# The products of the diffusion matrix in a two-layer graph kernel: one ordered list that runs ahead of its use, with the second step's results transposed and kept in DRAM

## The chip, the cores and the metric

The kernel runs on one core of one Trainium2 chip. The metric is the device time of the launch in microseconds. A profiled execution gives, besides, a trace of every instruction on the engines: TensorE (PE, matmuls and transposes; PEld is its weight load), VectorE (DVE), ScalarE (ACT), GpSimd (POOL) and SyncE (SP, which here only issues DMA transfers).

## The reference, cut to what matters

`x` is 2708x512 in fp32, `adj` 2708x2708 with entries 0 and 1. Layer 0 is a graph attention with 8 heads; it ends near 1050 us and neither kernel differs in it. Layer 1 is this, with `S = adj`, `U*` of 2x512x512 and `W*` projecting to 64 columns:

```python
S = S + eye(n)
Rf = S / clip(S.sum(axis=1, keepdims=True), 1e-12)
Rb = S / clip(S.sum(axis=0), 1e-12)[:, None]
Xf, Xb, Xa = (X, X, X)
Z = zeros_like(X)
for s in range(2):
    A = adj_from_feats(Xa, W1, W2, W3)      # logits (Xa W1) W2 (Xa W3)^T, then per row:
    Xf = Rf @ Xf                            # softmax, keep the largest entries up to a
    Xb = Rb @ Xb                            # mass of 0.9 (order decides ties), softmax
    Xa = A @ Xa                             # of what is kept
    Z = Z + (Xf @ U1[s] + Xb @ U2[s] + Xa @ U3[s])
Y = X + Z                                   # then a layer norm of Y; the layer's input is added
```

Both `Rf` and `Rb` are `S` with its rows scaled, so in step 1, where `Xf` and `Xb` are both `X`, one product `S @ X` serves both. In step 2 there are two, `S @ Xf` and `S @ Xb`.

## The kernel before, in words

**Tiles.** The 2708 rows are 22 row tiles of 128 (the last has 20). Two neighbouring tiles are a pair (`pairs`, 11), four are a quad (`quads`, 6, the last of two tiles). Each of the two steps is a pass over the pairs. Tiles are stored with 128 rows on the partitions.

**One pair in a step.** `Logits.queries` loads the queries; `Logits.products` (L517, L519) multiplies them with the resident `keys` and copies the logits to a tile `p` of 128x2708 (four buffers). `Logits.exp` gives the maxima (L544, VectorE), the exponentials in place (ACT), three thresholds to be looked at (`points`, GpSimd, which ends in the negated thresholds `nth`, L569) and, on ACT, two passes over `p` per threshold and tile, the looks (L549), which give the mass above it. `search` (VectorE) finds the threshold with further passes over `p` (`mass`, L624), writes the kept entries to `keep` and takes the largest of the rest (`finish`, L800 and L802), and branches at run time on whether ties or too few candidates need more work (L866 to L884); it ends in `rden`, the reciprocal of the kept mass (L901). `attended` transposes `keep` in groups of four blocks (L1004), copies them to `at` (L1008) and multiplies them with the resident values `va` (L1023); `rden` scales the result to `xa`. `mixed` (L1051) multiplies `xf`, `xb` and `xa`, each transposed first by `transposed` (L147, with the ACT copy at L149), with the blocks `u_k` of `U1`, `U2`, `U3`, which are loaded from DRAM every time. In step 1, `project` takes the transposed `xa` to next step's queries and keys in `kq_d`; the sum goes to `y_d`. In step 2, `y_d` is added and the layer norm follows: `moments` (L137 to L139) and two operations on VectorE in `normed` (L1083), and the store to `out`.

**`S`'s products.** `s_d` holds `S` transposed in DRAM. A product is computed in f32r with the right side split in two parts, `hl`, that sum to the fp32 value. `part(half, b)` returns a list of steps for half a quad. A step `product(c)` loads `hl` (L953, 512 KB) and a block `s_r` of `s_d` (L955, 256 KB) and issues two matmuls per row tile of the quad (L959) with 512 columns, into four PSUM tiles `q0` to `q3`. In step 1 one quad's 22 row blocks `c` are spread over two pairs; then `scaled` (L965) multiplies the result with 1/row sum and 1/column sum (`rinv`, `cinv`) on ACT, stores both to `xfb_d` (L966, issued by GpSimd) and calls `split_rows` (L181, L182 on VectorE; L183 stores to `fhl_d` or `bhl_d`), which makes the two parts for step 2. In step 2, `part` gives a quad's 22 blocks with `fhl_d` in one pair and with `bhl_d` in the next. `diffused` loads a pair's `xf` and `xb` from `xfb_d`.

**Order.** PE, ACT, DVE and SP run in the order in which the program issues (`manual_schedule`); GpSimd's order is set by a scheduler. While VectorE searches for pair g+1, the function `late` issues pair g's attention and `mixed` with two lists woven in by `paced`: `others` (the product steps) and `fills` (exponentials and looks of pair g+2). SP issues all loads in one order, and a load that waits for its buffer or its source holds those behind it.

**Start of a step.** Each step opens its own pools. It loads the keys, computes the first two pairs' logits, and runs eleven product blocks (step 1) or 22 (step 2) before `values` loads `va`, then more beside the first search. In step 2, `ranks` (L1099 to L1125) comes first: it gives each row its rank among rows with equal keys, for ties. It multiplies the keys with a ramp (L1103), copies to `same`, transposes, and counts with 22 passes of VectorE, eleven before the first logits and eleven after; `spread` sends the ranks to all partitions through DRAM.

Of the kernel before, what the change touches and what calls it, by code (L numbers as in the profile page):

```python
# [9 lines left out]
F32 = mybir.dt.float32  # L10
# [43 lines left out]
def kernel(  # L54
# [59 lines left out]
    xa_d = dram.tile([N, D], F32, name="xa_d")  # L114
    en_d = dram.tile([H, N], F32, name="en_d")
# [11 lines left out]
    ratio = const.tile([P, NT], F32, name="ratio")  # L127

# [13 lines left out]

    def transposed(pool, psum, src, pr, name):

        pt = psum.tile([P, KD, P], F32, name="t")
        for k in range(KD):
            nc.tensor.transpose(pt[:, k, :pr], src[:pr, k * P:(k + 1) * P], ident[:pr, :pr])  # L147
        dst = pool.tile([P, KD, P], F32, name=name)
        nc.scalar.copy(dst[:, :, :pr], pt[:, :, :pr])  # L149
        return dst  # L150
# [442 lines left out]
    def search(lg, looked, early, late):  # L593
# [110 lines left out]
        vn = small.tile([P, G, nx], F32, name="vn", bufs=1)  # L704
        sn = small.tile([P, G, nx], F32, name="sn", bufs=1)
        left = vec("left")
        eighth = small.tile([P, G, nx // 8], F32, name="eighth", bufs=1)
# [85 lines left out]
        def finish(go):  # L793
# [14 lines left out]
            rest = small.tile([P, G, nx], F32, name="rest", bufs=1)  # L808
# [95 lines left out]
    for s in range(STEPS):  # L904
        last = s == STEPS - 1
        with ExitStack() as st:
            big = st.enter_context(tc.tile_pool(name=f"s{s}big", bufs=1))
            wide = st.enter_context(tc.tile_pool(name=f"s{s}wide", bufs=2))
            sp = st.enter_context(tc.tile_pool(name=f"s{s}sp", bufs=4 if last else 3))
            work = st.enter_context(tc.tile_pool(name=f"s{s}work", bufs=2))  # L910
            up = st.enter_context(tc.tile_pool(name=f"s{s}u", bufs=4))
            parts = None if last else st.enter_context(tc.tile_pool(name=f"s{s}parts", bufs=2))
            small = st.enter_context(tc.tile_pool(name=f"s{s}small", bufs=2))
            ps_t = st.enter_context(tc.tile_pool(name=f"s{s}pst", bufs=2, space=PSUM))
            ps_a = st.enter_context(tc.tile_pool(name=f"s{s}psa", bufs=2, space=PSUM))
            ps_s = st.enter_context(tc.tile_pool(name=f"s{s}pss", bufs=1, space=PSUM))

            va = big.tile([P, NT, D], F32, name="va")

            keys = big.tile([P, N], F32R, name="keys")  # L920
            h = (NT - NT % G - G) * P
            for c in (slice(0, h), slice(h, N)):
                for i in range(2):
                    nc.sync.dma_start(out=keys[i * DA:(i + 1) * DA, c].bitcast(F32), in_=kq_d[s][:DA, i, c])
            rank = big.tile([P, N], BF16, name="rank") if last else None

            def values():
                for t in range(NT):
                    nc.sync.dma_start(out=va[:rows[t], t, :], in_=(xa_d if last else va_d)[cols[t], :])

            if last:
                g_b = big.tile([P, D], F32, name="g_b")
                nc.sync.dma_start(out=g_b, in_=row_bcast(gamma, D))

            def part(half, b):

                if b // 2 >= len(quads):  # L940
                    return []
                quad = quads[b // 2]
                first = b % 2 == 0
                w = len(quad) * P
                hl_d = (fhl_d if first else bhl_d) if last else vhl_d
                cs = range(NT) if last else range(0, NT // 2) if first else range(NT // 2, NT)
                steps = []

                def product(c):
                    if c == 0:  # L950
                        half[:] = [ps_s.tile([P, D], F32, name=f"q{i}") for i in range(len(quad))]
                    hl = sp.tile([P, 2, D], F32R, name="hl", bufs=3)
                    nc.sync.dma_start(out=hl.bitcast(F32), in_=hl_d[c * P:(c + 1) * P])  # L953
                    s_r = sp.tile([P, 2 * G * P], F32R, name="s_r")
                    nc.sync.dma_start(out=s_r[:, :w].bitcast(F32),  # L955
                                      in_=s_d[c * P:(c + 1) * P, quad[0] * P:quad[0] * P + w])
                    for j in range(len(quad)):
                        for h in range(2):
                            nc.tensor.matmul(half[j], lhsT=s_r[:, j * P:(j + 1) * P], rhs=hl[:, h],  # L959
                                             start=(c == 0 and h == 0), stop=(c == NT - 1 and h == 1))  # L960

                def scaled(t, ps, i, inv, to):
                    pr = rows[t]
                    x = work.tile([P, D], F32, name="xe")
                    nc.scalar.activation(x[:pr], ps[:pr], AF.Copy, scale=inv[:pr, t:t + 1])  # L965
                    nc.gpsimd.dma_start(out=xfb_d[i, cols[t], :], in_=x[:pr])  # L966
                    if not last:
                        split_rows(parts, nc.vector, x[:pr], t, to)

                steps += [lambda c=c: product(c) for c in cs]  # L970
                if last or not first:
                    for j, t in enumerate(quad):
                        if first or not last:
                            steps.append(lambda j=j, t=t: scaled(t, half[j], 0, rinv, fhl_d))
                        if not first:
                            steps.append(lambda j=j, t=t: scaled(t, half[j], 1, cinv, bhl_d))
                return steps

            def paced(steps, n):
                for step in steps[:n]:  # L980
                    step()
                del steps[:n]

            def diffused(grp):
                out_ = []
                for i in range(2):
                    for t in grp:
                        x = work.tile([P, D], F32, name=f"x{i}")
                        nc.sync.dma_start(out=x[:rows[t]], in_=xfb_d[i, cols[t], :])
                        out_.append(x)  # L990
                return out_[:len(grp)], out_[len(grp):]

            def attended(grp, keep, rden, fills, others, then):

                def turned(i, t, cs):
                    pr = rows[t]  # L1000
                    pt = ps_t.tile([P, TG, P], F32, name="t")
                    at = work.tile([P, TG, P], F32, name="at")
                    for j, c in enumerate(cs):
                        nc.tensor.transpose(pt[:rows[c], j, :pr], keep[i][:pr, cols[c]], ident[:pr, :pr])  # L1004
# [69 lines left out]
            def normed(t, y):  # L1074
# [10 lines left out]

                return rest

            def ranks():

# [148 lines left out]
```

## Time and profile before

| what | value |
|---|---|
| median of 3 runs | 3779.58 us (3772.61 to 3780.49) |
| the profiled execution | 3774.21 us, span of its instructions 3772.1 us |
| mean granted TensorE clock | 0.956 |
| layer 0, before 1050 us | PE busy 989.3, DVE 864.1, ACT 231.5, POOL 327.3 us |
| layer 1, step 1 (1050.0 to 2323.5 us) | PE 1101.8, DVE 636.4, ACT 655.5, POOL 254.6 us |
| layer 1, step 2 (2323.5 to 3772.0 us) | PE 1292.2, DVE 1110.7, ACT 653.1, POOL 256.4 us |
| DMA | 634 MB, 168 GB/s over the span; the DMA engines 50% busy |

The shares of busy time are averages over stages with different limits. The matmuls' ends in the trace are modelled and overlap, so the distance from one start to the next says more about a matmul's price than its listed duration. A group's line names the engine, the line of the kernel, output and input tiles, the count, then busy time and mean nanoseconds of one, then the idle time of the engine before the group and what ended it.

### The profile page before, as it was taken

Reading aid. Unit: us, or ns where it says so; the run is one execution under the profiler, and the core shown is the slowest. Engines: PE = TensorE matmul, PEld = TensorE weight load, DVE = VectorE, ACT = ScalarE, POOL = GpSimd, SP = SyncE. Lnnn points to the kernel's source line nnn. Section 1 sums busy time; section 2 is a strip of 40 time slices with the busy share of each in tenths; the row PEclk is TensorE's granted clock in tenths of the full one; section 3 lists DMA queues with packets and bytes.
Section 4 is the critical chain, followed back from the end, with each engine's and each line's share of the span. In section 5 each row is a group of like instructions: output and inputs, shape, how many; then the busy total and the mean of one; then the engine's idle time right before and its main releaser. Section 6 shows DMA issues by size and latency. Waiting matters only on the chain. (4 is left out here: it accounts for less than half of the span.)

```text
span 3772.1 us, 35425 instructions
## 1 busy us (share of the span) xinstructions
PE 3383.3 (90%) x11143; PEld 1760.6 (47%) x11143; DVE 2611.1 (69%) x4814; ACT 1540.1 (41%) x2334; POOL 838.2 (22%) x1187
## 2 busy tenths in 40 slices
PE   8999999999855898989898998668999999999988
PEld 4433333333533455545454453435555665556443
DVE  4588888989946526474554641967779798777992
ACT  2343202111025565546566621335544556445511
POOL 4115151423331121121212020302121211212101
PEclk9999999999977999999999998989999999999989
DMA  3476424233154554454545352845556665567552
GB/s 115 159 255 219 155 78 140 85 99 114 44 167 143 193 197 158 154 184 146 195 146 206 114 176 83 302 130 206 187 202 225 229 209 192 197 212 243 184 192 88
DMA packets 276457, 634.07 MB, mean 168 GB/s; under 512 B 37209, under 2 KB 70441, under 8 KB 273243
## 3 DMA queue, kind: packets, MB, share of 16 engines
q1 hardware_dynamic: 249183, 540.99, 43.3%
q0 software_dynamic: 27024, 90.30, 6.3%
q8 instruction: 89, 1.46, 0.2%
q14 instruction: 161, 1.32, 0.1%
HBM read 509.07 MB, written 122.10 MB: 167 GB/s over the span
## 5 line engine op out<-in xcount | busy, mean ns | idle before, releaser
L1023 PE MATMUL a<-va,at 128*128 128x512 f32 (+2 forms) x1936 | 898.0, 603 | 58.0 <-ACT at L1008 57.9
L959 PE MATMUL q<-hl,s_r 128*128 128x512 f32 x2904 | 821.8, 429 | 67.2 <-DMA s_r<-s_d 65.7
L429 PE MATMUL po<-e,fw 128*65 128x512 f32 (+4 forms) x2112 | 840.4, 553 | 30.0 <-DVE e L427 22.2
L427 DVE SCALAR_TENSOR_TENSOR e<-r_b,kk,a_c 128x512 f32<-128x512 f32 (+4 forms) x1056 | 752.3, 741 | 68.8 <-PE po L429 18.2
L959 PEld LDWEIGHTS q<-hl,s_r 128*128 128x128 f32 x2904 | 545.8, 190 | 312.4 <-issue 147.5
L549 ACT ACTIVATE junk_a<-p,nth 128x2708 uint8<-128x2708 f32 (+1 forms) x240 | 613.0, 2554 | 93.2 <-POOL nth L569 89.6
L429 PEld LDWEIGHTS po<-e,fw 128*65 128x65 f32 (+1 forms) x2112 | 286.5, 140 | 544.2 <-issue 269.1
L1023 PEld LDWEIGHTS a<-va,at 128*128 128x128 f32 (+2 forms) x1936 | 339.6, 188 | 428.2 <-issue 347.2
L1051 PE MATMUL a<-u_k,v_t 128*128 128x512 f32 (+1 forms) x1056 | 490.8, 601 | 20.9 <-ACT xa L1031 15.1
L624 DVE SCALAR_TENSOR_TENSOR junk<-p,th 128x2708 bf16<-128x2708 f32 (+1 forms) x132 | 402.2, 3047 | 4.0
L1008 ACT COPY at<-t 128x512 f32<-128x512 f32 (+3 forms) x308 | 139.8, 476 | 439.4 <-PE t L1004 439.2
L1051 PEld LDWEIGHTS a<-u_k,v_t 128*128 128x128 f32 (+1 forms) x1056 | 188.6, 186 | 239.6 <-issue 187.0
L517 PE MATMUL t<-keys,q_t 128*128 128x452 f32 x528 | 167.9, 444 | 117.0 <-ACT p L519 95.0
L800 DVE SCALAR_TENSOR_TENSOR keep<-p,th 128x2708 f32<-128x2708 f32 (+1 forms) x44 | 133.4, 3033 | 132.4 <-PE t L1004 131.1
L181 DVE TENSOR_SCALAR split_hl<-xe 128x512 int32<-128x512 int32 (+1 forms) x44 | 19.0, 432 | 275.6 <-ACT xe L965 232.6
L802 DVE MAX8 vn<-keep 128x8 f32<-128x2708 f32 (+1 forms) x66 | 196.8, 2981 | 2.3
L519 ACT COPY p<-t 128x452 f32<-128x452 f32 (+2 forms) x264 | 132.7, 539 | 149.8 <-DVEq L884 78.9
L517 PEld LDWEIGHTS t<-keys,q_t 128*128 128x128 f32 x528 | 91.8, 211 | 188.7 <-ACT p L519 149.5
L411 ACT ACTIVATE s_c<-a_c 128x512 fp32r<-128x512 f32 (+3 forms) x132 | 76.2, 577 | 248.3 <-DMA a_c<-in_adj_t_dram 123.2
L1004 PE MATMUL t<-ident,keep 128*128 128x128 f32 (+1 forms) x968 | 146.4, 273 | 21.9 <-DVE keep L752 16.5
L1004 PEld LDWEIGHTS t<-ident,keep 128*128 128x128 f32 (+1 forms) x968 | 114.5, 138 | 105.1 <-issue 76.9
L544 DVE TENSOR_REDUCE nmx<-p 128x1 f32<-128x2708 f32 (+1 forms) x44 | 129.2, 2966 | 40.3 <-ACT p L519 40.1
(294 smaller groups left out, 3105.1 us busy)
## 6 DMA issues: line engine op xcount, KB each, us to landing
s_r<-s_d SPq DMA_DIRECT2D x330, 256.0 KB
hl<-vhl_d SPq DMA_DIRECT2D x132, 512.0 KB
u_k<-in_L_gnn_U_dram SPq DMA_DIRECT2D x264, 256.0 KB
hl<-fhl_d SPq DMA_DIRECT2D x132, 512.0 KB
hl<-bhl_d SPq DMA_DIRECT2D x132, 512.0 KB
arow<-in_adj_dram SPq DMA_DIRECT2D x21, 1354.0 KB
s_d<-s_c SPq DMA_DIRECT2D x88, 256.0 KB
a_c<-in_adj_t_dram SPq DMA_DIRECT2D x84, 256.0 KB
```

The costliest lines, as they stand in the source:

```text
L427: nc.vector.scalar_tensor_tensor(e[:pr, :cw], r_b[:pr, i, :cw], kk[:pr, t, hd:hd + 1], a_c[t][:pr, :cw], op0=OP.max, op1=OP.mult)
L429: nc.tensor.matmul(po[i][:, :cw], lhsT=fw[:pr, t, hd, :], rhs=e[:pr, :cw], start=(t == 0), stop=(t == NT - 1))
L517: nc.tensor.matmul(pl[:, :c1 - c0], lhsT=q[:, i], rhs=self.keys[:, c0:c1], start=(i == 0), stop=(i == 1))
L549: nc.scalar.activation(junk[:pr], self.p[i][:pr], func, **kw)
L624: v.scalar_tensor_tensor(junk_b[:pr], ps_[i][:pr], th, ps_[i][:pr], op0=OP.is_ge, op1=OP.mult, accum_out=dst)
L800: v.scalar_tensor_tensor(keep[i][:pr], ps_[i][:pr], t, ps_[i][:pr], op0=OP.is_lt, op1=OP.mult, accum_out=left[:pr, i:i + 1] if e else None)
L802: v.max(vs, keep[i][:pr])
L959: nc.tensor.matmul(half[j], lhsT=s_r[:, j * P:(j + 1) * P], rhs=hl[:, h], start=(c == 0 and h == 0), stop=(c == NT - 1 and h == 1))
L1004: nc.tensor.transpose(pt[:rows[c], j, :pr], keep[i][:pr, cols[c]], ident[:pr, :pr])
L1008: nc.scalar.copy(at[:r, j0:j1, :pr], pt[:r, j0:j1, :pr])
L1023: nc.tensor.matmul(pa[:pr], lhsT=at[:rows[c], j, :pr], rhs=va[:rows[c], c, :], start=(c == 0), stop=(c == NT - 1))
L1051: nc.tensor.matmul(pz[i][:rows[t]], lhsT=v_t[i][:, k, :rows[t]], rhs=u_k, start=(n == 0 and k == 0), stop=(n == 2 and k == KD - 1))
```

## The change

A class `Products` holds one list of steps for both passes: in step 1's part per quad 22 `product` and one `scaled` per tile, in step 2's part per quad and per side (`Xf`, `Xb`) 22 `turned` and four `stored`. There are 466 steps. The driver takes a number of them for each pair, whichever pass they belong to. Two sets of 26 (one quad each) are taken at the start of step 1, before and beside the first search. The rest is spread over step 1's pairs so that step 2 keeps 32 for its start and 19 for each of ten pairs.

`turned` exchanges the operands of the matmul, so that the result comes out transposed, 512 row numbers of the quad along the free side. `stored` copies it to `xt_d` in DRAM without a scale. `diffused` loads it for a pair in step 2 and multiplies it, with `times` on GpSimd, by a row of `rinv` or `cinv` that `spread_scales` has written to `scale_d` and that is broadcast to all partitions. In step 1 `xb` is no longer transposed: it is the transposed `xf` times `ratio`. `split_rows` is gone from the products: `split` loads a stored tile from `xfb_d`, multiplies by 4097, subtracts twice for the upper part and once for the lower, all on GpSimd; seven splits are issued per pair in step 1.

The last pair of step 1 transposes and projects `xa` first; its `u` products, in the order `U3`, `U1`, `U2`, are issued in step 2's start. `ranks` becomes a class `Ranks` whose tiles are two of the `p` buffers: the keys of the first 18 tiles are loaded, and their ranks counted, beside the last pair of step 1; the other four tiles follow after the last keys. The pools are opened once for both steps; `s_r` has three buffers in both (before: 3 and 4), `u_k` three (3 and 4), the shared tiles `v_t` take both row tiles of a pair. Layer 0 is as before.

```diff
-            def part(half, b):
-                ...
-                cs = range(NT) if last else range(0, NT // 2) if first else range(NT // 2, NT)
-                ...
+        class Products:
+            def __init__(self):
+                self.steps, self.ready, self.splits, self.split_at = [], {}, [], 0
+                self.at = 0
+                for q, quad in enumerate(quads):
+                    self.steps += [lambda quad=quad, c=c: self.product(quad, c) for c in range(NT)]
+                    self.steps += [lambda t=t, j=j: self.scaled(t, j) for j, t in enumerate(quad)]
+                    self.ready[0, q] = len(self.steps)
+                for q, quad in enumerate(quads):
+                    for i in range(2):
+                        self.steps += [lambda quad=quad, i=i, c=c: self.turned(quad, i, c) for c in range(NT)]
+                        self.steps += [lambda quad=quad, q=q, i=i, k=k: self.stored(quad, q, i, k)
+                                       for k in range(KD)]
+                    self.ready[1, q] = len(self.steps)
+            ...
+            def turned(self, quad, i, c):
+                while (i, c) not in self.splits[:self.split_at]:
+                    self.split(1)
+                hl, s_r, w = self.operands((fhl_d, bhl_d)[i], quad, c)
+                for k in range(KD):
+                    for h in range(2):
+                        nc.tensor.matmul(self.half[k][:, :w], lhsT=hl[:, h, k * P:(k + 1) * P], rhs=s_r[:, :w],
+                                         start=(c == 0 and h == 0), stop=(c == NT - 1 and h == 1))
+
+            def stored(self, quad, q, i, k):
+                w = len(quad) * P
+                x = work.tile([P, D], F32, name="xe")
+                nc.scalar.copy(x[:, :w], self.half[k][:, :w])
+                nc.gpsimd.dma_start(out=xt_d[q, i, :, k, :w], in_=x[:, :w])
+
+            def split(self, n):
+                for i, t in self.splits[self.split_at:self.split_at + n]:
+                    self.split_at += 1
+                    ...
+                    nc.gpsimd.dma_start(out=x, in_=xfb_d[i, cols[t], :])
+                    nc.gpsimd.tensor_scalar(x4[:pr], x, 4097.0, None, op0=OP.mult)
+                    nc.gpsimd.tensor_tensor(high, x4[:pr], x, op=OP.subtract)
+                    nc.gpsimd.tensor_tensor(high, x4[:pr], high, op=OP.subtract)
+                    nc.gpsimd.tensor_tensor(x, x, high, op=OP.subtract)
+                    nc.gpsimd.dma_start(out=(fhl_d, bhl_d)[i][t * P:(t + 1) * P], in_=hl)
...
+        def times(dst, v, r, i, w):
+            nc.gpsimd.tensor_tensor(dst[:, :, :w], v[:, :, :w], r[:, i, :w].unsqueeze(1).to_broadcast([P, KD, w]),
+                                    op=OP.mult)
...
+                x = up.tile([P, KD, G * P], F32, name="v_t")
+                nc.sync.dma_start(out=x[:, :, :w], in_=xt_d[q, i, :, :, c0 * P:c0 * P + w])
+                times(x, x, r, i, w)
...
+        BEGUN, AHEAD = 32, 19
...
+                if not s:
+                    load_keys(0, 0, known * P)
+                    load_keys(0, known * P, N)
+                else:
+                    load_keys(1, known * P, N)
+                    ...
+                    paced(rest_of_first, 1)
...
+                if s:
+                    ranks.counted(known, NT)
...
+                paced(rest_of_first, len(rest_of_first))
+                first = NT + 2 * G if not s else BEGUN // 2
+                steps = S.take(first)
+                paced(steps, first // 2)
+                lg[1].products()
+                if not s:
+                    spread_scales()
+                paced(steps, first)
+                values(s)
...
+                    if not s and g > 0:
+                        S.split(7)
...
+                    if g < 0:
+                        n = BEGUN - first if s else NT + 2 * G
+                    elif not s:
+                        n = -(-(total - 10 * AHEAD - BEGUN - S.at) // (NP - g))
+                    else:
+                        n = -(-(total - S.at) // (NP - 1 - g)) if g < NP - 1 else 0
+                    others = S.take(n)
...
+                            if final:
+                                v_a = turned_rows(grp, xa)
+                                asked(grp, v_a)
+                                vf = turned_rows(grp, xf)
+                                vb = by_columns(vf)
+                                three = mixed(s, grp, (2, 0, 1), (lambda: v_a, lambda: vf, lambda: vb), others, fills)
+                                rest_of_first.extend(three)
+                                return
...
+                        if not s:
+                            load_keys(1, 0, known * P)
+                            ranks = Ranks()
+                            others.insert(min(8, len(others)), lambda: ranks.sums(0, known))
...
+                        if not s:
+                            ranks.counted(0, known)
```

## The prediction

> **What bounds the kernel now.** I read the page's engine line, then TensorE's timeline where nothing waits, for the price of one matmul; then the windows, cut at the first transposes of each pair's attention; then what TensorE and VectorE wait for in them.
>
> ```profile
> PE 3383.3 (90%) x11143; PEld 1760.6 (47%) x11143; DVE 2611.1 (69%) x4814; ACT 1540.1 (41%) x2334; POOL 838.2 (22%) x1187
> ```
> TensorE (PE) looks like the bound, but the share doesn't say in which stage it waits.
>
> ```profile
> 2646.64 1.88 PE L1051 MATMUL a<-u_k,v_t 128*128 128x512 f32 x4
> 2647.95 2.42 PE L959 MATMUL q<-hl,s_r 128*128 128x512 f32 x8
> 2650.20 1.88 PE L1051 MATMUL a<-u_k,v_t 128*128 128x512 f32 x4
> ```
> First column: start. From the first start to the third, 4 f32 and 8 f32r matmuls take 3.56 us: 0.429 for an f32 one (each f32 product shows as two) and 0.23 for an f32r one. Elsewhere in that timeline starts of transposes lie 0.109 apart, of `project` 0.112, of the logits' matmuls 0.206. So a pair of step 1 asks of TensorE 44x0.109 (transposes of `keep`, `L1004`) + 88x0.429 (`L1023`) + 24x0.109 (`L147`) + 48x0.429 (`L1051`) + 16x0.112 + 24x0.206 + 88x0.229 (`S`, `L959`) = 92.6 us. A pair of step 2 has 176 at `L959` and no `project`: 111.0.
>
> ```profile
> 1450.60:1549.00 98.40, 96.39 (x333) 53.97 (x333) 60.85 (x131) 59.78 (x75) 13.91 (x27) 1.00 0.43 140
> 1549.00:1664.00 115.00, 99.28 (x333) 55.62 (x333) 52.18 (x119) 64.58 (x83) 29.53 (x50) 0.94 0.54 187
> 2323.50:2531.60 208.10, 124.93 (x463) 85.21 (x462) 154.23 (x245) 80.18 (x104) 44.55 (x44) 0.85 0.67 220
> 3017.30:3134.00 116.70, 114.04 (x405) 68.97 (x405) 92.28 (x181) 61.72 (x75) 20.95 (x28) 1.00 0.63 210
> ```
> Columns: stretch, length, busy PE, PEld, DVE, ACT, POOL, then clock, DMA share, GB/s. A quiet pair takes its demand plus 5.7 us (98.4 and 116.7). Every second pair of step 1 takes 112 to 115: those whose `scaled` steps put `split_rows` on VectorE. `finish` stands behind the splits there, and the next logits stand behind `finish`:
>
> ```profile
> 1643.26 1.46 PE L517 MATMUL t<-keys,q_t 128*128 128x452 f32 x4
> 1655.69 4.61 PE L517 MATMUL t<-keys,q_t 128*128 128x452 f32 x10 [10.97 <-ACT p L519]
> ```
> The third window is the turn from step 1 to step 2: TensorE's demand there is 104 us of 208.
>
> ```profile
> 2338.98 1.09 PE L1103 MATMUL t<-keys,s_r 128*128 128x452 f32 x2 [15.44 <-DMA keys<-kq_d]
> 2361.94 2.09 PE L959 MATMUL q<-hl,s_r 128*128 128x512 f32 x8 [0.87 <-DMA s_r<-s_d]
> 2579.97 3.75 PE L959 MATMUL q<-hl,s_r 128*128 128x512 f32 x8 [17.09 <-DMA s_r<-s_d]
> ```
> The keys make a round trip through DRAM (15.4); then VectorE counts ranks and searches. Products alone go at the pace of their loads: from 2355.4, 22 steps of 768 KB in 55.9 us, 2.54 each against 1.83 of matmuls.
>
> ```profile
> 3106.59 0.14 DVE L881 TENSOR_SCALAR code_i<-code 1x1 int32<-1x1 f32 x1
> 3113.74 0.17 DVE L901 RECIPROCAL rden<-den 128x2 f32<-128x2 f32 x1 [7.00 <-issue]
> 3126.34 0.69 DVE L137 BATCH_NORM_STATS2 ln_st<-yo 128x6 f32<-128x512 f32 x1 [12.44 <-POOL yo L1068]
> ```
> This limits what step 2 can win: VectorE goes from one pair's moments (3009.7) to `rden` (3113.7) in 104 us, 97 of work and 7 at the branch, and then has only 12.4 us to spare.
>
> **What the skill says.** *GPSIMD Engine Reference*, "Elementwise": a two-input elementwise operation costs about 2.6 cycles per element at 1.2 GHz, 1.1 us for 512 elements; the trace is slower, 1.3 to 1.6 us per 128x512, and I use the trace. *SBUF — State Buffer*, "Who interferes with whom": a VectorE instruction with two SBUF inputs contends with GpSimd's reads; that fits the slower figure, no run here separates it. *DMA: Bandwidth & Descriptors*, "Issuing engines are not separate DMA queues": transfers that GpSimd issues share the same 16 engines; the trace moves 296 GB/s in the 55.9 us above at a DMA share of 88%, so a faster stream of products has little room there.
>
> **The change, part by part.** Sums are against the profiled execution (span 3772.1, 3774.21 with what lies around it, 5.4 below the median 3779.58). `S`'s products count in steps: one step is one row block `c`, 8 matmuls. A quad is four row tiles; six quads, the last of two tiles.
>
> *Matmuls.* Step 2's products become 1760 at 512 columns and 352 at 256, for 1936 at 512. No row shows 256 columns; the logits' 452 take 0.206, so 0.11 to 0.23; I take 0.125: 403 + 44 us for 443, +4. 88 transposes of `xb` leave step 1, 176 of `xf` and `xb` leave step 2: 264x0.109 = 29 us off TensorE. Their ACT copies (0.57 each) go too; ACT is no bound.
>
> *Start of step 1.* The list takes 44 product steps ahead of the first pair, for 22. Loads set it: 44x2.5 = 110 us, then `va` 18 us (5.5 MB), from 1103 to about 1234; VectorE, which set it before, is done by 1190. The 16 scaled copies go through two `xe` buffers whose stores land after 3.0 us, 8x3 = 24 us, and SP holds loads behind the `scale_d` stores for some 4: 1262. GpSimd now does the splits:
>
> ```profile
> L182 POOL TENSOR_TENSOR split_hl<-v,split_hl 128x512 f32<-128x512 f32 (+1 forms) x22 | 33.3, 1512 | 2.0 <-DVE split_hl L181 1.5
> L966 POOL DMA_DIRECT2D xfb_d<-xe x88 | 51.4, 585 | 424.6 <-ACT xe L965 402.1 <-DMA va<-xa_d 17.1 <-ACT p L519 2.3
> ```
> One split is four operations of about 1.45 and two issues of 0.57: 6.9 us; all 44 are 300 us. In the built order the points of the third pair's search stand behind eight of them (55 us). ACT's looks wait for these points, the copies to `at` stand behind the looks, TensorE waits for `at`: with the slack that the first pair leaves, I take 22 us, bounds 0 and 55. The first pair's demand is 104.6, so the second starts at 1262 + 104.6 + 5.7 + 22 = 1394, where it started at 1338.8: **55 us later**, with 29 more product steps done (53 us of matmuls).
>
> *Pairs 2 to 10 of step 1.* By the built order TensorE's demand is 861.9 us (40 to 144 `S` matmuls a pair), and 9x5.7 = 51. The stalls of every second pair (57 us in all) go, since no split is left on VectorE. What is late next is GpSimd: the thresholds `nth` behind three splits (11 us, one pair), the `ratio` product that makes `xb` behind eight splits (7 us, two pairs), copies to `xe` whose stores stand behind a split (4 quads, 2 each): 33; I take 30, bounds 5 and 70. 862 + 51 + 30 = 943 for 912: **31 later**, 60 more product steps done.
>
> *The turn.* The last pair projects first; its `u` products (48x0.429 = 20.6) fill the keys' round trip. Twenty-two rank counts become 18 beside that pair, where VectorE has room (42 us busy in the pair before), and 4 after the keys (11.7 us). From the last project: keys 15.5, ranks and logits 11, maxima, exp and points 18, so the first masses at +45 (before +67), the search's 114 as before, +159; the second pair's search ends about +273, since `keep` is free only when the first pair's transposes are done. The last pair of step 1 reaches its project in 82 + 5. Together 360 us for 409, from its first transposes to those of step 2's second pair: **49 earlier**. SP holds the `u_k` loads behind the waiting keys (10 us); that lies inside the wait for the keys.
>
> *Pairs 2 to 10 of step 2.* TensorE's demand falls from 111 to 96 to 104 (79 to 85 in the last three), 102 to 109 with the 5.7. VectorE's chain stays at 104 us (117.7 and 119.5 in the two pairs with ties, 98 in the last) and becomes the bound: 104 + 118 + 105 + 104 + 104 + 111 + 104 + 120 + 98 = 968 for 1034, **66 earlier**, where TensorE alone would give 143. The loads of `xt_d` and their scaling on GpSimd (two of about 3 us per pair) are asked for a pair's attention ahead: nothing; without that cover 5 us a pair. The last pair has 16 transposes fewer: **2**.
>
> Sum: -55 - 31 + 49 + 66 + 2 = 31 earlier: 3743 for the profiled execution, **3748** for the median.
>
> **Rivals.** *GpSimd's work hides* (0.27): splits fall where nothing waits. Against 3748 the start gains 20 (copies not held) and 22 (looks), the pairs 25: 3681. For it: GpSimd is busy 22%. Against: ACT already waits 89.6 us for `nth`. If VectorE's branch overlapped in step 2, a further 10: 3670; the trace never shows that.
> *GpSimd becomes the bound* (0.21, the slower side): every pair of step 1 with splits waits for `nth` or `ratio`. Seven or eight splits are 48 to 55 us of a 100 us pair; if they hold each of six pairs for 15 to 20 us, the 30 becomes 90 to 110: 3815. It turns to slower at 61 us, or 10 a pair.
> *It moves work and nothing more* (0.07): what leaves step 2 costs as much in step 1, and VectorE's bound eats the rest: 3775 to 3785.
>
> **Numbers.** About 0.2% (7.5 us) can be told from no change. Main case 0.45, own range 3722 to 3771. Faster 0.27 + 0.43 = 0.70; same 0.08; slower 0.22. The range, 3670 to 3802, reaches from the best case of the first rival to where half of the slower one begins.
>
> **What would show it.** Windows of step 1 near 100 to 110 with no alternation, and the wait at the logits gone; the first attention near 1262; splits of 6 to 7 us on GpSimd; ACT waiting longer for `nth` than 89.6 us; in step 2 pairs of 104 to 106, VectorE with under 2 us before the moments, and TensorE waiting for `keep` or `p`. If step 2's pairs are 98 or less, VectorE's chain isn't what I read; if pairs of step 1 that hold splits are over 115, the GpSimd rival holds.

## The result, and the profile after

The changed kernel takes 3905.68 us (median of 4 runs, 3899.57 to 3911.06), the kernel before 3778.40 (3772.61 to 3780.49): a ratio of 1.0339, 95% interval 1.0316 to 1.0362. The profiled execution took 3910.51 with a span of 3908.7, 136.6 above the span before. Cut at the first transposes of the pairs' attention, as in the prediction:

| stage | before | after | predicted |
|---|---|---|---|
| up to the second pair of step 1 | 1338.8 | 1438.2 | 1394 |
| pairs 2 to 10 of step 1 | 912.0 | 1024.7 | 943 |
| turn (last pair, first pair of step 2) | 416.5 | 364.7 | 360 |
| pairs 2 to 10 of step 2 | 1023.1 | 996.3 | 968 |
| last pair | 81.6 | 84.9 | 80 |

(For before, the prediction has 409 and 1034 in rows three and four; no one cut gives both. Summed over this table, its forecast is 27 us earlier than before, not 31.) The turn came out near its forecast, and step 2 got shorter; the start and step 1 lost far more.

The page's engine line: TensorE's busy time is almost the same as before, GpSimd's half as long again.

```profile
PE 3388.9 (87%) x11058; PEld 1755.4 (45%) x11058; DVE 2678.3 (69%) x4727; ACT 1503.9 (38%) x2275; POOL 1216.0 (31%) x1447
```

Windows of the changed kernel, columns as before (length, PE, PEld, DVE, ACT, POOL, clock, DMA share, GB/s): two pairs of step 1 with splits, the last pair with the turn, and a quiet pair of step 2.

```profile
1438.20:1580.70 142.50, 108.33 (x349) 60.86 (x349) 56.57 (x112) 63.58 (x81) 77.45 (x87) 0.88 0.51 175
1816.00:1943.40 127.40, 97.62 (x300) 51.25 (x300) 58.80 (x112) 63.38 (x81) 79.08 (x87) 0.88 0.53 181
2462.90:2716.00 253.10, 188.46 (x644) 103.96 (x642) 161.13 (x264) 90.41 (x131) 60.69 (x67) 0.89 0.61 202
3285.50:3388.70 103.20, 99.61 (x333) 56.64 (x333) 93.75 (x167) 59.16 (x71) 29.09 (x30) 1.00 0.57 190
```

Where splits run, GpSimd is busy 77 to 79 us (14 in a quiet pair before) and the pair takes 127 to 143 us for a TensorE demand of 86 to 97. The granted clock is 0.88 in these two and 1.00 in the quiet pair, but starts of the matmuls of `L1111` lie 0.429 us apart in all three (medians), so slower matmuls are not the loss. In the quiet pair of step 2 VectorE is busy for 93.75 of 103.2 us. Over pairs 2 to 10 of step 2 it waited 78 us for the layer norm's sums before the change and 15 after (line that waited, what it waited for, us in total, times, longest):

```profile
DVE ln_st L137 <- POOL yo L1068: 78.0, 14, 14.8
```
```profile
DVE ln_st L143 <- POOL yo L1163: 15.4, 7, 10.1
```

TensorE's timeline shows the long waits of the start and of the first pairs:

```profile
1200.91 3.33 PE L982 MATMUL q<-hl,s_r 128*128 128x512 f32 x7 [21.91 <-DMA s_r<-s_d]
1293.70 8.16 PE L514 MATMUL t<-keys,q_t 128*128 128x452 f32 x20 [22.24 <-ACT p L516]
1367.47 5.85 PE L1111 MATMUL a<-va,at 128*128 128x512 f32 x8 [23.53 <-ACT at L1096]
1553.34 2.92 PE L1147 MATMUL a<-u_k,v_t 128*128 128x512 f32 x3 [18.14 <-POOL v_t L1056]
```

The first is the load of `va` ahead of the second quad's operands. The second is ACT, which stood at that quad's copies to `xe`: a copy needs a buffer whose store has landed, and GpSimd issued these stores behind a split. The third is ACT as well: its looks had to wait for `nth`, and the copies to `at` stood behind the looks. The last is GpSimd: `ratio` times `v_t` stood behind splits. ACT's lines for the second and the third:

```profile
1281.63 0.69 ACT L989 ACTIVATE xe<-q,rinv 128x512 f32<-128x512 f32 x1 [11.08 <-DMA xfb_d<-xe]
```
```profile
1363.72 2.55 ACT L546 ACTIVATE junk_a<-p,nth 128x2708 uint8<-128x2708 f32 x1 [30.58 <-POOL nth L566]
```

GpSimd's timeline shows why its work was late:

```profile
1227.05 1.49 POOL L1020 TENSOR_SCALAR x<-split_hl 128x512 f32<-128x512 f32 x1 [6.35 <-DMA split_hl<-xfb_d]
...
1301.11 3.90 POOL L1020 TENSOR_SCALAR x<-split_hl 128x512 f32<-128x512 f32 x1
1305.09 3.02 POOL L1021 TENSOR_TENSOR split_hl<-x,split_hl 128x512 f32<-128x512 f32 x1
...
1358.42 0.61 POOL L1024 DMA_DIRECT2D bhl_d<-split_hl  x1 [0.30 <-POOL split_hl L1023]
...
1363.44 0.25 POOL L566 TENSOR_SCALAR nth<-th_a 128x6 f32<-128x6 f32 x1
```

It waits in its own order for the tile that it has asked for; some operations take 3 to 4 us instead of 1.3 to 1.5; and `nth` of the third pair comes only after the sixteenth split. The groups of the splits' rows (busy time and mean, then idle time ahead):

```profile
L1020 POOL TENSOR_SCALAR x<-split_hl 128x512 f32<-128x512 f32 (+1 forms) x44 | 82.3, 1869 | 63.2 <-DMA split_hl<-xfb_d 62.2
L1021 POOL TENSOR_TENSOR split_hl<-x,split_hl 128x512 f32<-128x512 f32 (+1 forms) x44 | 68.7, 1562 | 3.2
L1023 POOL TENSOR_TENSOR split_hl<-split_hl 128x512 f32<-128x512 f32 (+1 forms) x44 | 61.4, 1395 | 2.7
L1022 POOL TENSOR_TENSOR split_hl<-x,split_hl 128x512 f32<-128x512 f32 (+1 forms) x44 | 56.0, 1272 | 3.2
L1019 POOL DMA_DIRECT2D split_hl<-xfb_d x44 | 25.7, 585 | 23.3 <-DMA xfb_d<-xe 17.5 <-DMA fhl_d<-split_hl 4.5 <-POOL split_hl L1017 0.6
```

Arithmetic 268 us, issues of loads and stores 51, waits in between 101 (with 5.8 at the stores): 420 us over 44 splits, 9.6 each, where the prediction had 6.9.

### The profile page after: what moved, and what is told of

It is laid out like the page before. It is cut to its first block, busy times and chain, and to the rows that moved or that the text cites. A ratio compares the mean times of both kernels' runs of the same rounds, so it can differ in the third digit from the quotient of the medians.

```text
span 3908.7 us, 35336 instructions
## 1 busy us (share of the span) xinstructions
PE 3388.9 (87%) x11058; PEld 1755.4 (45%) x11058; DVE 2678.3 (69%) x4727; ACT 1503.9 (38%) x2275; POOL 1216.0 (31%) x1447
## 5 line engine op out<-in xcount | busy, mean ns | idle before, releaser
L1111 PE MATMUL a<-va,at 128*128 128x512 f32 (+2 forms) x1936 | 910.6, 610 | 73.6 <-ACT at L1096 73.3
L999 PE MATMUL q<-s_r,hl 128*128 128x512 f32 (+1 forms) x2112 | 550.4, 409 | 75.3 <-ACT xe L1005 38.0
L1111 PEld LDWEIGHTS a<-va,at 128*128 128x128 f32 (+2 forms) x1936 | 344.5, 190 | 455.1 <-issue 354.3
L1147 PE MATMUL a<-u_k,v_t 128*128 128x512 f32 (+1 forms) x1056 | 491.2, 608 | 58.3 <-POOL v_t L1056 25.2
L999 PEld LDWEIGHTS q<-s_r,hl 128*128 128x128 f32 x2112 | 381.3, 193 | 239.2 <-issue 92.6
L621 DVE SCALAR_TENSOR_TENSOR junk<-p,th 128x2708 bf16<-128x2708 f32 (+1 forms) x132 | 414.6, 3141 | 4.0
L982 PE MATMUL q<-hl,s_r 128*128 128x512 f32 x968 | 275.8, 435 | 77.6 <-DMA s_r<-s_d 58.8
L982 PEld LDWEIGHTS q<-hl,s_r 128*128 128x128 f32 x968 | 188.8, 199 | 158.6 <-issue 67.6
L514 PE MATMUL t<-keys,q_t 128*128 128x452 f32 x528 | 159.6, 426 | 97.0 <-ACT p L516 76.1
L1056 POOL TENSOR_TENSOR v_t<-v_t,scales 128x1024 f32<-128x1024 f32 (+1 forms) x33 | 117.0, 3555 | 226.6 <-ACT v_t L1044 183.3
```

The costliest lines, as they stand in the source:

```text
L514: nc.tensor.matmul(pl[:, :c1 - c0], lhsT=q[:, i], rhs=self.keys[:, c0:c1], start=(i == 0), stop=(i == 1))
L621: v.scalar_tensor_tensor(junk_b[:pr], ps_[i][:pr], th, ps_[i][:pr], op0=OP.is_ge, op1=OP.mult, accum_out=dst)
L982: nc.tensor.matmul(self.half[j], lhsT=s_r[:, j * P:(j + 1) * P], rhs=hl[:, h], start=(c == 0 and h == 0), stop=(c == NT - 1 and h == 1))
L999: nc.tensor.matmul(self.half[k][:, :w], lhsT=hl[:, h, k * P:(k + 1) * P], rhs=s_r[:, :w], start=(c == 0 and h == 0), stop=(c == NT - 1 and ...
L1111: nc.tensor.matmul(pa[:pr], lhsT=at[:rows[c], j, :pr], rhs=va[:rows[c], c, :], start=(c == 0), stop=(c == NT - 1))
L1147: nc.tensor.matmul(pz[i][:rows[t]], lhsT=v_t[:, k, i * P:i * P + rows[t]], rhs=u_k, start=(n == 0 and k == 0), stop=(n == 2 and k == KD - 1))
```

## The experiments

My theory after this: GpSimd's splits make `nth`, the `ratio` products and the stores of `xe` late (start and step 1), and slow VectorE beside them; the longer start is itself a loss; step 2 is bound by VectorE. Rivals: the product steps moved into step 1 are the loss, whoever splits; the round trip through DRAM alone is; TensorE still bounds step 2. All medians of "before" beside the runs lay between 3775.1 and 3778.7. Stages in us of each profiled execution, same cuts (steps ahead are the product steps left for each pair of step 2, 19 in the changed kernel):

| kernel | time | to 2nd pair | step 1, 2-10 | turn | step 2, 2-10 |
|---|---|---|---|---|---|
| changed | 3905.7 | 1438.2 | 1024.7 | 364.7 | 996.3 |
| splits on VectorE | 3854.5 | 1446.3 | 959.4 | 365.2 | 1001.4 |
| splits without arithmetic | 3829.7 | 1406.5 | 976.7 | 365.9 | 998.9 |
| short start | 3888.9 | 1378.9 | 1055.4 | 368.5 | 999.0 |
| start alone as before | 3866.0 | 1356.1 | 1053.2 | 369.2 | 1001.1 |
| 12 steps ahead | 3995.7 | 1442.5 | 1098.3 | 372.8 | 996.0 |
| no scaling in step 2 | 3876.7 | 1427.9 | 1026.9 | 355.1 | 980.1 |
| turn undone | 3943.3 | 1429.6 | 1019.8 | 407.8 | 999.7 |
| VectorE splits, short start, 19 | 3873.4 | 1413.8 | 1004.0 | 372.2 | 999.6 |
| the same, 22 | 3856.1 | 1407.5 | 981.6 | 370.8 | 1015.5 |
| the same, 25 | 3837.9 | 1404.6 | 954.9 | 363.4 | 1036.0 |
| combined | 3789.0 | 1349.5 | 953.2 | 364.2 | 1033.4 |
| even pairs | 3751.6 | 1341.7 | 919.5 | 375.9 | 1033.7 |

"No scaling" and "turn undone" leave the code of the start as it is, and still have it 10 and 9 us shorter than the profiled execution of the changed kernel (which is 5 us above its median). A single stage that differs by some 10 us is no finding.

**Splits on VectorE.** `scaled` calls `split_rows`; `turned`'s loop and `S.split(7)` go.

```diff
-                    self.splits.append((i, t))
+                    split_rows(parts, nc.vector, x[:pr], t, (fhl_d, bhl_d)[i])
```


> The changed kernel with one part undone: each scaled tile is split at once on VectorE (two operations, 1.1 us) from xe, as before the change; nothing is split on GpSimd and nothing is read back from DRAM for it. Theory (GpSimd's splits make the thresholds nth, the ratio products and the stores of xe late, and slow VectorE's passes that run beside them): the first pair starts some 15 us sooner, its 23.5 us wait at `at` goes, the pairs 2 to 10 of step 1 lose 60 to 90 of their 113 us; VectorE's extra 43 us of step 1 shrinks to under 15. Total 3905 less 90 to 120: 3785 to 3815. Rival (the longer start and the 60 product steps moved into step 1 are the loss, whoever splits): 3870 to 3900.

Measured 3854.46 (ratio to before 1.0202, 1.0185 to 1.0219), between the ranges of theory and rival. The pairs lose 65 us, as the theory said, and ACT's wait for `nth` falls. The groups of the looks, of the changed kernel and of this one:

```profile
L546 ACT ACTIVATE junk_a<-p,nth 128x2708 uint8<-128x2708 f32 (+1 forms) x240 | 612.8, 2553 | 192.3 <-POOL nth L566 188.5
```
```profile
L546 ACT ACTIVATE junk_a<-p,nth 128x2708 uint8<-128x2708 f32 (+1 forms) x240 | 612.7, 2553 | 126.1 <-POOL nth L566 122.3
```

VectorE's excess in pairs 2 to 10 of step 1 (what its instructions took beyond the median of their line and form, summed over those that start beside a GpSimd operation of more than 1 us) falls from 43 us to 16. So the moved steps are not the whole loss: they are still there. They may be part of it, since these pairs still take 47 us more than before the change; the runs with 22 and 25 steps ahead bear on that. The first attention came at 1335.6, 34 later instead of 15 sooner, behind a new wait in the start, and the total missed its range:

```profile
1327.70 4.62 PE L514 MATMUL t<-keys,q_t 128*128 128x452 f32 x10 [68.02 <-ACT p L516]
```

**Splits without arithmetic.**

```diff
-                    nc.gpsimd.tensor_scalar(x4[:pr], x, 4097.0, None, op0=OP.mult)
-                    ... (three subtractions)
+                    nc.gpsimd.dma_start(out=high, in_=xfb_d[i, cols[t], :])
```


> The changed kernel with the arithmetic of the splits left out: GpSimd still loads each stored tile (into both halves, two issues) and stores it, in the same places, but computes nothing, so step 2's products of S are of wrong parts. Theory A (the four GpSimd operations of a split, 5.3 us and more beside VectorE, are what is late): 3905 less 60 to 100. Theory B (the round trip through DRAM in GpSimd's own order, 3 us for the load and 3 for the store, is): 3905 less 0 to 25.

3829.7 (one run), 76 of the 127 us less: theory A. The arithmetic on GpSimd is the larger part of the cost. The round trip isn't shown to be free: pairs 2 to 10 still take 17 us more than with splits on VectorE.

**The start: two versions.** First the second 26 steps left out of the start (`n = ... else 0`), then the start as before the change:

```diff
-                first = NT + 2 * G if not s else BEGUN // 2
+                first = NT // 2 if not s else BEGUN // 2
-                        n = BEGUN - first if s else NT + 2 * G
+                        n = BEGUN - first if s else NT + 2 * G - first
```
(with `values(s)` moved ahead of `spread_scales()`).

> The changed kernel with the second 26 steps of the start left to the ten pairs (2 to 3 more each). Theory (a product step costs about the same in the start, where its loads set it, as in a pair): first attention 60 to 70 us sooner, pairs of step 1 together 35 to 60 us longer, total 3905 less 0 to 30. Rival (the pairs have idle TensorE that would take the steps for nothing, the start was pure loss): 3905 less 55 to 70.

> The changed kernel with the start alone set back (11 steps, then the values, then 15 beside the first search; splits stay on GpSimd, 19 steps ahead). Theory (44 product steps ahead of the first pair go at the pace of loads, and the copies to xe at the pace of stores; after 22 of them VectorE's first search sets the start as before): first attention 1200 to 1225, second pair 1330 to 1365, pairs of step 1 as in the short start (1055): total 3905 less 40 to 70. Rival (GpSimd's splits hold the start whatever its length): first attention 1255 or later, less than 25 off.

Short start 3888.86, start as before 3865.95 (one run each). The second pair starts 59 and 82 us sooner, the pairs lose 31 and 29 of it again, since they take the steps. So a step costs more in the start than in a pair, but is no pure loss: the theory, with its sizes short. The first attention came 37 us sooner (60 to 70 expected) and at 1227.5 (1200 to 1225), the totals are 17 and 40 less. In the short start ACT held the first attention. Its looks of the second pair waited for `nth` behind splits, and the copies of the third pair's logits, due ahead of that attention, stood behind the looks:

```profile
1225.24 2.55 ACT L546 ACTIVATE junk_a<-p,nth 128x2708 uint8<-128x2708 f32 x1 [20.76 <-POOL nth L566]
```

In the changed kernel these looks end at 1267, only 4 us ahead of the start's last product, so a shorter start alone could not give the whole 60 to 70. With the start as before, `nth` comes ahead of the splits (the same wait is 6.8 us). The changed kernel's second set in the start, in a window, and the transfers of GpSimd's queue then (count, size, median us to landing):

```profile
1200.90:1271.50 70.60, 50.95 (x180) 37.20 (x180) 1.07 (x11) 41.83 (x35) 43.57 (x52) 0.90 0.91 317
```
```profile
fhl_d<-split_hl POOLq DMA_DIRECT2D x4, 512.0 KB, 7.8
split_hl<-xfb_d POOLq DMA_DIRECT2D x6, 256.0 KB, 5.0
...
xfb_d<-xe POOLq DMA_DIRECT2D x2, 256.0 KB, 7.2
```

The 22 product steps take 70.6 us, 3.2 each, at a DMA share of 0.91, with VectorE idle; the transfers of the splits are in flight then, and land in 5 to 8 us where a store of `xe` took 3.0 before (median of the run). The run with splits on VectorE has the same 22 steps with GpSimd's loads for the splits gone:

```profile
1200.50:1258.80 58.30, 46.10 (x177) 32.58 (x178) 45.92 (x82) 16.10 (x14) 6.99 (x15) 0.98 0.95 327
```

They take 58.3 us there, 2.65 each, and 71.5 us in the run without arithmetic, which keeps the transfers: these are worth 12 us.

**Twelve steps ahead** (`AHEAD = 12`).

> The changed kernel with 12 instead of 19 product steps left for each pair of step 2; 70 more are done in step 1. Theory (VectorE's chain of 104 to 108 us bounds step 2's pairs): pairs 2 to 10 of step 2, 996 us now, change by less than 25; step 1 grows by 60 to 130; total 3950 to 4020. Rival (TensorE with its waits bounds them): they lose 90 to 120 us, total 3880 to 3930.

Windows over the nine pairs of step 2, first of this run, then of the changed kernel:

```profile
2913.60:3909.60 996.00, 810.22 (x2564) 430.57 (x2564) 896.06 (x1612) 470.05 (x557) 219.85 (x241) 0.90 0.38 126
```
```profile
2827.60:3823.90 996.30, 878.32 (x3005) 499.65 (x3005) 895.62 (x1611) 474.15 (x565) 243.76 (x249) 0.95 0.52 171
```

TensorE has 441 matmuls less in it; the time is the same to 0.3 us, and VectorE's work to 0.5. So TensorE doesn't bound step 2 at 19 steps a pair. That VectorE's chain does is read from its own waits: in the changed kernel 15 us for the layer norm's sums, under 1 for TensorE, and 41 at run-time branches, beside 895.6 us of work. Step 1 pays 74 us and gets nothing back; total 3995.7 (one run), inside its range.

**No scaling in step 2** (`times(x, x, r, i, w)` left out).

> The changed kernel with the scaling of the loaded columns in step 2 left out (20 GpSimd products of about 3.4 us; step 2's Xf and Xb lack their row scales). Theory (they slow VectorE's instructions beside them, which is why its chain is 107 and not 104 us): VectorE's work per quiet pair falls from 100 to 96 or 97 us, pairs 2 to 10 of step 2 lose 20 to 40 of 996 us. Rival (the chain is longer for another reason, the waits for xe or for the layer norm's sums): less than 10.

```profile
2809.90:3790.00 980.10, 876.18 (x3005) 500.35 (x3005) 859.00 (x1612) 475.04 (x565) 174.35 (x229) 0.95 0.52 173
```

VectorE's work falls from 895.6 to 859.0 us (854.6 in the same pairs before): GpSimd's 20 products did slow it. The stretch loses 16, short of the 20 expected; the turn is 10 shorter, which may be chance. The rest of the 37 us became idle time of VectorE: 10 us more at the layer norm's sums, 9 more for TensorE's transposes of `keep`.

**The turn undone** (`final = False`; `Ranks()`, its `sums` and all 22 `counted` after the keys in step 2's start).

> The changed kernel with the last pair's part undone: its U products stay in step 1, ahead of its projection as for other pairs, and all ranks are made in step 2's start from keys loaded there at once (22 counts of VectorE instead of 4 after the keys). Theory (20.6 us of U products filled the keys' round trip, and 18 counts of about 1.6 us lay beside the last pair): the turn, 364.7 us from the last pair's first transposes to those of step 2's second pair, grows by 40 to 55, total 3945 to 3960. Rival (search and loads set the turn anyway): it grows by less than 15.

The turn grows by 43 us (40 to 55 expected), the total to 3943.27 (one run, 2 us under its range): the theory.

**Both parts undone, and the number of steps ahead.** VectorE's splits with the short start, `AHEAD` 19, 22 and 25.

> The changed kernel with two parts undone together: splits on VectorE from xe, and only the first 26 steps in the start. Theory (VectorE's second set of splits in the start, which came late after their loads, was the 68 us wait of the run with splits on VectorE): that wait goes, the second pair starts near 1350, the pairs 2 to 10 of step 1 take 990, the rest as in the changed kernel: 3780 to 3805. Rival (what holds the start is the search itself or the values' loads, whoever splits): 3830 to 3860.

> As the run with both parts undone, with 22 instead of 19 product steps left for each pair of step 2. Theory (TensorE bounds step 1's pairs, VectorE's chain of about 107 us bounds step 2's, so that a step costs 1.83 us in step 1 and nothing in step 2 as long as TensorE's demand there stays under some 101 us): step 1 loses 40 to 55, step 2 grows by 5 to 25; 20 to 45 less than with 19. Rival (TensorE's time is the same wherever the step is): within 8 us of it.

> The same with 25. Theory: step 1 loses 80 to 110 against 19, step 2's pairs are bound by TensorE again (demand 107 to 113 and 5.7) and grow by 50 to 80: 15 to 50 less than with 19, about the same as with 22. Rival (TensorE's time is the same wherever the step is): within 8 us of it.

The first expectation failed: 3873.35, above the rival's range too, and the second pair starts at 1413.8. TensorE waits 91.9 us at the third pair's logits. VectorE's timeline of this run:

```profile
1177.30 0.43 DVE L178 TENSOR_SCALAR split_hl<-xe 128x512 int32<-128x512 int32 x1 [68.46 <-ACT xe L989]
```

VectorE stands 68 us at the first split, which waits for the whole first quad; the first search, whose thresholds were there by 1122 in the changed kernel, is issued behind it. So even the first eight splits were in the wrong place, not only the second set. With 22 and 25 the time falls to 3856.10 and 3837.87: step 1 gets 22 and 49 us shorter (40 to 55 and 80 to 110 expected), step 2 gets 16 and 36 longer (5 to 25 and 50 to 80). The 17 us for 22 are short of the 20 expected, the 35 for 25 inside; the rival, no difference, falls. For 25 the pairs hold 100 steps' matmuls instead of 142, so a step left out of them saves 1.2 us, less than its 1.83 us of matmuls.

**Combined, and even pairs.** Splits on VectorE, the start as before the change, 25 ahead; then the scales sent after the first search, 26 ahead, and 13 steps for each pair:

```diff
-                        n = -(-(total - 10 * AHEAD - BEGUN - S.at) // (NP - g))
+                        n = (15 if not g else 13) if g < NP - 1 else total - 10 * AHEAD - BEGUN - S.at
```


> The changed kernel with three parts set back: splits on VectorE from xe; the start as before (11 steps, then the values, then 15 beside the first search, so that VectorE meets the first splits after that search); 25 product steps left for each pair of step 2. What stays of the change is one list, transposed products of step 2, the last pair's U products and the ranks moved. Theory (the wait of 90 us at the start came from splits that stand ahead of the first search on VectorE): second pair near 1345, pairs 2 to 10 of step 1 near 955, the rest as with 25 before: 3837 less 50 to 75, 3760 to 3790 us. Rival (the start is set by loads and the values): 3820 to 3840.

> As the combined run (splits on VectorE, start as before), with three settings: the rows of scales are sent out after the first search, not ahead of its loads; 26 steps left for each pair of step 2; in step 1 fifteen steps for the first pair, 13 for each further one (16 in the last), so that each quad's copies and splits come in the second half of an odd pair. Theory (in the combined run the copies to xe stand early in a pair and wait for splits that stand behind VectorE's search; even demand leaves 878 us and some 40 of such waits): first attention 1215 to 1235, pairs 2 to 10 of step 1 905 to 930 (953 there), total 3740 to 3770, under the kernel before. Rival (the waits come wherever a quad ends, since VectorE is then in its search): 940 or more, total 3770 to 3790.

Combined: 3788.95 (1.0034, 1.0022 to 1.0047), at the upper end of its range; the second pair starts at 1349.5, as the theory said. Its pairs still wait where splits stand early in a pair: an ACT line of the run with 25 ahead, which has the same steps per pair, shows a copy to `xe` behind VectorE's search.

```profile
2087.99 0.69 ACT L989 ACTIVATE xe<-q,rinv 128x512 f32<-128x512 f32 x1 [21.75 <-DVE split_hl L179]
```

Even pairs: 3751.57 us, ratio **0.9933** (0.9919 to 0.9946), faster than both kernels. Pairs 2 to 10 of step 1 take 919.5 (expected 905 to 930), and each wait at the end of a quad is short:

```profile
1403.90 1.22 PE L982 MATMUL q<-hl,s_r 128*128 128x512 f32 x2 [5.62 <-ACT xe L989]
```

The first attention, 1235.8, was just above its range. That the quads' ends stand better is not shown to be the cause: pairs 2 to 10 lose 34 us against the combined run, and 24 of them are TensorE's busy time (869.8 to 845.7), since they hold twelve steps fewer. TensorE's waits for copies to `xe` add up to 37 us, not less than the combined run's 27; its waits for `at` fell from 30 to 13.

What the kernel keeps of the change is the list, the transposed products and the turn. Against the kernel before, only the turn is shorter, by 41 us; the start and pairs 2 to 10 of steps 1 and 2 are 3, 7.5 and 11 us longer.

## Why the prediction was wrong

It said 31 us faster, with a range of 3670 to 3802; the measured time is 127 us slower, above the range. The step that failed is the cost of the work that moved to GpSimd: a split was priced by its instructions, 6.9 us, and took 9.6 with its waits; its transfers and the scaling in step 2 were put at nothing. In their place the runs showed pairs 2 to 10 of step 1 at 82 us over the forecast (65 us go with the splits on VectorE), 12 us for the transfers in the start, and 37 us more work of VectorE in step 2. The second rival (GpSimd becomes the bound) named this cause and the side, but at 3815 not the size.

- **Start (55 late; measured 99).** The 22 us for the looks were right, mechanism and size: TensorE waited 23.5 at `at`, since `nth` stood behind the second eight splits. VectorE was done by 1201, near the 1190 said. What failed is the sum that leads to the first attention: 1302, not 1262. Its "44x2.5 = 110 us" left out that the splits' transfers use the same DMA engines: the second 22 steps took 3.2 us each, 12 us more than without these transfers. The logits of the second and the third pair stand in the same stretch, 8.6 and 8.3 us, and are in no term; the other differences are smaller. The place cited from the Trainium skill's *DMA: Bandwidth & Descriptors* says that transfers of all issuing engines share the same DMA engines; I drew it for `S`'s stream and not for the splits.
- **Pairs of step 1 (31 longer; measured 113).** The stalls at the logits did go (TensorE waited there 40 us before, 10.5 after). But the trace has 992 matmuls of `S` in these pairs and 704 before: 36 more steps of eight, not 60, and with the prediction's own prices 872 us of demand, not 862. With its 51 around them that leaves 102 us of stalls, where it took 30 (bounds 5 and 70). The mis-sized term is the price of a split, 6.9 us for 9.6, and with it how many waits follow: splits without arithmetic give back 48 us here, splits on VectorE 65. The prediction's 1.1 us for 512 elements is an estimate from the cycles that *GPSIMD Engine Reference*, "Elementwise", states; undisturbed the trace has 1.26 to 1.29 for the two-input operations, and 3.0 to 3.6 at times beside VectorE. VectorE's own operations got longer beside the splits too, which the prediction had cited and not priced.
- **Turn (360; measured 364.7).** Right, and shown by undoing it (43 us). That it came so close is in part luck: the last project ended after 78 us, where 87 were said, and VectorE's search ended 170 us behind it, where 159 were said.
- **Step 2 (968; measured 996).** That VectorE becomes the bound was right: twelve steps ahead and VectorE's waits show it. Its chain was not 104: the work of these nine pairs rose from 854.6 to 895.6 us beside the products with `scales`, which I had costed at nothing. Leaving them out gives 980; the other 12 us I did not take apart. TensorE waited there for copies to `xe` (14.1 us in one pair), which may be part of it.
- **The matmuls.** Starts of the products at 256 columns lie 0.120 us apart, of those at 512 0.23: 0.125 was near enough.
- **The range.** Its upper end treated the start, step 1 and step 2 as separate costs. They missed together, by 44, 82 and 28 us, and GpSimd's new work is shown as the cause of a part of each: 12, 48 to 65, and 16.

A point missed before any price: since VectorE bounds step 2, steps taken out of it for step 1 bought less there than they cost. From 25 to 19 steps a pair step 2 gains 36 us and step 1's pairs pay 49; from 19 to 12 step 2 gains nothing and they pay 74.

## What to carry to other kernels

Work that is moved to an engine with little to do is not free: ask what else that engine must deliver and stand the new work behind it, with its waits for DMA in the engine's own order. Before moving work out of a stage, find which engine ends it once that work is gone; here no run brought pairs 2 to 10 of step 2 from 1023 us below 980, whatever left TensorE, and steps beyond that only lengthened the other stage. Undo the parts of a change one by one: here only the turn is seen to save time. Where an engine runs in order, the place of a few short instructions can cost more than their work: eight splits of 1.1 us ahead of a search held VectorE for 68 us.

## What the runs showed of the hardware

VectorE and GpSimd hold each other up for whole instructions. A VectorE operation on 128x2 elements, 0.161 us at the median, took 2.18 us in the changed kernel while GpSimd ran two products of 128x1024, from 3177.05 to 3187.13; the view of that line over the whole run gives minimum, median and maximum, and the same line before the change (`L673`) never took over 0.3:

```profile
3184.97 2.18 DVE L670 TENSOR_TENSOR fr<-top,cur 128x2 f32<-128x2 f32 x1
```
```profile
3177.05 10.08 POOL L1056 TENSOR_TENSOR v_t<-v_t,scales 128x1024 f32<-128x1024 f32 x2 [5.19 <-DMA v_t<-xt_d]
```
```profile
L670 DVE TENSOR_TENSOR fr<-top,cur x66: 160/161/2185, 1151.4 to 3771.0; 128x2 f32<-128x2 f32 x66
```

It goes the other way too: GpSimd's `th_a` on 128x6 takes 0.2 us at the median and up to 3.06, about the length of one of VectorE's passes over `p` (3.04). This is what the Trainium skill's *SBUF — State Buffer*, "Who interferes with whom", calls an exclusive lock, held for the whole instruction; the trace agrees: the 2.18 us end 0.02 us after GpSimd's products. Who waits is not fixed: before the change VectorE's passes lost nothing in step 2 (`mass`, 3.04 us, beside GpSimd's work as alone), and GpSimd's small operations were the ones that took long (`L576` on 128x6, ten in that step at 2.2 us).
